# A four-layer convolution and scan kernel: sort comparisons placed by a table, evictions before convolution taps, weight sums in more scan slots, and one activation table for a norm

## The chip, the cores and the metric

The kernel runs on one core of a Trainium2 chip. Its five compute engines appear in the profile as PE (TensorE: matrix products and transposes), DVE (VectorE), ACT (ScalarE), POOL (GpSimd) and SP (SyncE, which here only issues DMAs). The metric is the time of one execution on the device in microseconds. Before the change the median of three executions is 2826.08 us (2825.05 to 2827.95).

## The reference

The input x is one image of 1024 channels and 64 x 64 places, in float32. Four layers follow one another, each added to its input after a group norm over 32 groups:

```python
x = x + L0(gn(x))   # a scan over channels with learned decay
x = x + L1(gn(x))   # 1x1 convolution, 1024 -> 1024, bias
x = x + L2(gn(x))   # gated state-space layer, below
x = x + L3(gn(x))   # 1x1 convolution, 1024 -> 1024, bias
```

Layer 2 is the long one:

```python
xz = silu(in_proj_w @ x + in_proj_b)        # 3072 x 1024 weights
x_ssm, res, gate = split(xz, 3)
xf = silu(conv3(x_ssm))                     # depthwise, 3 taps along the 4096 places
perm = per head, argsort of the score of a Moebius map of the 64 x 64 grid
dt, B, C = split(dbc_w @ xf + dbc_b)        # gathered by perm, as xf is
y = selective_scan(xf[perm], dt, A, B, C)   # two heads, 8 states, 4096 steps
y = y[inverse of perm] * silu(gate) + res
out = silu(out_proj_w @ y + out_proj_b)
```

What is sorted depends on the input `mobius`, so the kernel sorts 4096 keys for each of the two heads on the chip.

## The kernel before, in words

**Products.** A 1024 x 1024 weight matrix times 1024 x 4096 values is worked in four pairs of blocks of 512 columns. Each pair is a 2 x 2 block product in seven products (Strassen's scheme with sums of blocks of the weights and of the values), in two groups of rows, so 14 products a pair. The index `i % 14` in the code is the place of a product in its pair: 0 to 6 for the first group, 7 to 13 for the second. One product is 16 matmuls of 128 x 128 by 128 x 512 (L787) into two PSUM banks of one of two tags, A and B; `put` and `add` carry the banks out (L885 and L889 in the pointwise layer), and a bank can't be written anew before that. The operands of the next pair (b21, b11, b22, then the sums t1 to t4, L745) are made during the last places of a pair, on DVE, and for t2 to t4 on POOL. Sums of weight blocks are made once, on POOL (sum_weights, sum_weights2: L426, L435, L446, L453), stored to DRAM, and loaded again as weights.

**The order of work.** Nearly all stages lie in `tc.manual_schedule` blocks: in these, each engine executes its instructions in the order in which the program issues them. Outside of them the compiler's scheduler chooses. Generators are stepped by hand: after each product, the loop takes one step of whatever runs beside it. So the line at which a step is called sets what stands in front of what on each engine's queue[...].

**The stages**, with their place in the profiled span: layer 0 (0 to 225 us); the pointwise layer 1 (230 to 633, loop at L914); the norm of layer 2 (to 639); the convolution stage, where the first third of the input projection (WX) is followed by the 3-tap convolution, the transposes into token order and the dt/B/C product (639 to 1129, loop at L1108 to L1129, and a tail to 1167); the scan in 74 steps (1180 to 1720, loop L1242 to L1278), with the products of the second third (WR) woven in, 14 a pair again; the gate and output projections (1722 to 2455, two_steps); the norm of layer 3 (to 2474); layer 3 itself (two_steps, to the end).

**The sort** is a bitonic network of 78 comparisons (`compare`, L295 to L319: 11 DVE instructions on tiles of 64 x 128 each), and ten turns of the tile (`turn_over`: two transposes on PE at L329 into a PSUM buffer, and a copy on ACT at L331), after which a permutation goes to DRAM through POOL. It is a generator that yields "compare" or "turn" ahead of each such part; `sort_on` (L373) is called after each product of layer 1 and of the convolution stage, and takes up to n steps. In layer 1 it does so in places 4 to 12, if no sum of weights is under way (`quiet`); in the convolution stage in places 4 to 12, or everywhere from the product 45 on.

**PSUM for transposes.** `ps_tp` (L95) gives out two buffers of one tag, "tp", in turn. The sort's transposes, the norms' small matmuls and the turns of the convolution stage share them: the next user of a buffer waits until the last reader of its former content is done.

**The convolution stage.** After each product, `follow` (L1037) takes two finished blocks of x_ssm through the convolution: `conv` (ACT first tap L973 into a PSUM tile cvp, then two taps on DVE, L976), then silu on ACT (L1047). One call later, `turn` (L986) transposes and multiplies a block by `both` in two halves of two tiles (eight matmuls, L995, into two tp buffers), each half carried out by ACT (l2xt, L997), summed on POOL (L1003) and stored by SP. One of the two blocks turned in a cycle is taken in the middle of the next product (`turn(*due3.pop(0))`), the other in `follow`. ACT also makes the b operands of the next pair (L871), the put and silu of the products' results (L1019, L1028).

**The scan's end.** In each scan step a slot at L1268 lets POOL take one step of the weight sums for WO and W3, except in the places 11 and 12 of a pair of WR; what is left over is done after the last step. Results of WR go through silu and are stored to `res_d` by SP (`activate`, L942 to L948, four at a time). The gate stage begins by reading blocks x_x_b (ACT's queue, L1325), normed into qb (L1332); its first copies out of PSUM are L1497.

**The norm of layer 3** (L1548) has eight aggregations of statistics (L178), two small matmuls (L192, L199), and a logarithm and an exponential for the root (L166, L167).

Of the kernel before, what the change touches and what calls it, by code (L numbers as in the profile page):

```python
# [88 lines left out]
def tile_net(ctx: ExitStack, tc: tile.TileContext, x, par_d, cst_d, w_d, w2_d, dbcw_d, out):  # L89
    nc = tc.nc  # L90
# [29 lines left out]
    def pcol(name, i, rows=P):  # L120
        at = PAR[name].start + i
        return par[:rows, at : at + 1]
# [58 lines left out]
    def group_norm(name):  # L181
        return finish_of(norm_steps(name, *moments(name)))
# [187 lines left out]

    coming = [None]

    def sort_on(quiet, n=2):  # L373

        for _ in range(n):
            was = coming[0]
            if was is None or (was == "compare" and not quiet):
                return
            coming[0] = next(order, None)
            if "turn" in (was, coming[0]):  # L380
                return
# [529 lines left out]
    with tc.manual_schedule(engines={E_.DVE, E_.PE, E_.Pool, E_.Activation}):  # L911
        for i, _ in enumerate(pointwise("l1", W1, "b1", [3, 2] + EARLY, x0_d, x1_d)):
            busy = next(sums, None) if i % 14 < 13 else None
            sort_on(not busy and 3 < i % 14 < 13)  # L914
        for _ in sums:
            pass
    sum_pool.__exit__(None, None, None)
# [32 lines left out]
    with tc.tile_pool(name="l2a", bufs=2) as pa, tc.tile_pool(name="l2a2", bufs=1) as pa2, \  # L950
# [14 lines left out]
        def conv(o, nb):  # L965
            side = nb % 2
            xo = xs[o]
            n = f"{o}_{nb}"
            cv = psa.tile([P, FB], F32, tag="cv", name=f"cvp{n}", bufs=2)
            if side == 1:  # L970
                nc.vector.tensor_copy(carry[:, o, :], xo[:, 2 * FB :])
            at = side * FB
            nc.scalar.activation(cv, xo[:, at : at + FB], AF.Identity, bias=pcol("dwb", o),  # L973
                                 scale=pcol("dww", 3 * o))
            for t in (1, 2):
                nc.vector.scalar_tensor_tensor(cv, xo[:, at + t : at + t + FB], pcol("dww", 3 * o + t), cv,  # L976
                                               ALU.mult, ALU.add)
            if nb == NB - 1:
                e = end[:, o : o + 1]
                nc.vector.tensor_scalar(e, xo[:, 2 * FB : 2 * FB + 1], pcol("dww", 3 * o), pcol("dwb", o),  # L980
                                        ALU.mult, ALU.add)
                nc.vector.scalar_tensor_tensor(e, xo[:, 2 * FB + 1 :], pcol("dww", 3 * o + 1), e,
                                               ALU.mult, ALU.add)
            return o, nb, cv

        def turn(o, nb, cv):  # L986
            pair, side = divmod(nb, 2)
            h, c0 = o // KH, (o % KH) * P
            t0 = nb * FB - 1
            n = f"{o}_{nb}"  # L990
            xt = pa.tile([P, TPB, NV], F32, tag="xt", name=f"l2xt{n}", bufs=3)
            for q0 in (0, 2):
                pt = ps_tp(f"l2pt{n}_{q0}")[:, : 2 * NV]
                for q in range(2):
                    nc.tensor.matmul(pt[:, q * NV : (q + 1) * NV], cv[:, (q0 + q) * P : (q0 + q + 1) * P],  # L995
                                     both[:, o, :], start=True, stop=True)
                nc.scalar.copy(xt[:, q0 : q0 + 2, :].rearrange("p q c -> p (q c)"), pt)  # L997
            if pair not in accs:
                accs[pair] = pa.tile([P, 2 * TPB + 1, HEADS * NF], F32, tag="acc", name=f"acc{pair}", bufs=2)
            acc = accs[pair][:, side * TPB : (side + 1) * TPB, :]  # L1000
            old = acc if nb in done else dbcb.unsqueeze(1).to_broadcast([P, TPB, HEADS * NF])
            done[nb] = True
            nc.gpsimd.tensor_tensor(acc, xt[:, :, P:], old, ALU.add)  # L1003
            xt = xt[:, :, :P]
            if nb == 0:
                nc.sync.dma_start(tok_d[h * N : h * N + P - 1, c0 : c0 + P], xt[1:, 0, :])
                nc.sync.dma_start(tok_rows(t0 + P, TPB - 1, P, c0, h), xt[:, 1:, :])
            else:
                nc.sync.dma_start(tok_rows(t0, TPB, P, c0, h), xt)
# [12 lines left out]
        have, ready, due, due2, due3 = set(), [], [], [], []  # L1022
# [14 lines left out]
        def follow():  # L1037


            made = [conv(*c) for c in due]  # L1040
            for c in due3:
                turn(*c)
            due3[:] = due2
            due2[:] = []
            for o, nb, ps in made:
                cv = pa.tile([P, FB], F32, tag="cv", name=f"cv{o}_{nb}", bufs=4)
                nc.scalar.activation(cv, ps, AF.Silu)  # L1047
                due2.append((o, nb, cv))
            due[:] = ready[:CONVS]
            del ready[:CONVS]  # L1050
# [58 lines left out]
        with tc.manual_schedule(engines={E_.DVE, E_.PE, E_.Pool, E_.Activation}):  # L1109
            nc.sync.dma_start(both[:, :, P:], dbcw_d)  # L1110
            nc.gpsimd.tensor_copy(both[:, :, :P], ident.unsqueeze(1).to_broadcast([P, CT, P]))
            nc.gpsimd.memset(row, 0.0)
            ends, i = iter(()), -1
            for half in run(EARLY + LATE, [WX], normed(norm2), put2a, add2a, before2,
                            last_eng=nc.vector, fine=True, tell=True):
                if half:
                    if due3:
                        turn(*due3.pop(0))
                elif half is False:
                    follow()  # L1120
                if half is not None:
                    continue
                i += 1
                if i > 14 and i % 14 == 4:
                    ends = finish(i // 14 - 1)
                next(ends, None)
                sort_on(3 < i % 14 < 13 or i > 44)
            while coming[0] is not None:
                sort_on(True)  # L1129

            forget(EARLY)
            units = run([3, 2] + EARLY, [WR], normed(norm2), put2b, add2b, before2, fine=True, B=last_B[0])
            total, first, given = NP * 2 * NG * 7, 11, 0

            def next_units(upto):
                nonlocal given
                if given < upto:
                    given += 1
                    next(units, None)

            while ready or due or due2 or due3:
                follow()
                for _ in range(2):
                    next_units(6)
                activate(len(silus))
            for _ in finish(NP - 1):
                pass
# [5 lines left out]
    with tc.tile_pool(name="l2r2", bufs=8) as prg, tc.tile_pool(name="l2g", bufs=5) as pgat, tc.tile_pool(name="l2b", bufs=2) as pb, tc.tile_pool(name="l2h", bufs=1) as ph, \  # L1153
# [88 lines left out]
        with tc.manual_schedule(engines={E_.DVE, E_.PE, E_.Pool, E_.Activation}):  # L1242
            while given < first:
                next_units(total)
            for k in range(4):
                gather(k)
            step_sums(0)
            for k in range(-1, NK + 1):
                upto = first + (k + 2) * (total - first) // (NK + 2)
                turned = turn_rows(k + 1) if k + 1 < NK else None  # L1250
                if k > 0:
                    weigh(k - 1, pgs.pop(k - 1))
                if turned is not None:
                    spread_decay(k + 1, *turned)
                if k + 2 < NK:
                    step_sums(k + 2)
                next_units(upto)
                y = apply(k - 1) if k > 0 else None
                if 0 <= k < NK:
                    pgs[k] = cross(k)  # L1260
                if k + 1 < NK:
                    nc.scalar.activation(decay_[k + 1], decay_[k + 1], AF.Exp)
                if y is not None:
                    scatter(k - 1, y)
                if 3 < k + 4 < NK:
                    gather(k + 4)
                next_units(upto)
                if given // 2 % 14 not in (11, 12):  # L1268
                    next(sums, None)
                if len(silus) > 3:  # L1270
                    activate(4)
            while given < total:
                next_units(total)
            next(units, None)
            while silus:
                activate(4)
            for _ in sums:
                pass  # L1278
# [266 lines left out]

    with tc.manual_schedule(engines={E_.DVE, E_.PE, E_.Pool, E_.Activation}):
        two_steps([job for pair in range(NP) for job in (("gate", WG, pair), ("out", WO, pair))], norm2, x1_d)
    norm3 = group_norm("gn3")  # L1548
    with tc.manual_schedule(engines={E_.DVE, E_.PE, E_.Pool, E_.Activation}):
        two_steps([("last", W3, pair) for pair in range(NP)], norm3, x2_d)  # L1550

# [101 lines left out]
```

## Time and profile before

| | before |
|---|---|
| median of three executions | 2826.08 us |
| profiled execution, its own time | 2827.72 us |
| span of the profile | 2825.9 us |
| PE busy | 2639.0 us (93%) |
| DVE, ACT, POOL busy | 1779.7, 1093.2, 1294.2 us |
| mean granted clock of TensorE | 0.971 |
| PE busy in 230 to 639 (layer 1) | 393.3 of 409 us |
| PE busy in 639 to 1180 (convolution) | 510.3 of 541 us |
| PE busy in 1180 to 1722 (scan) | 526.1 of 542 us |
| PE busy in 1722 to 2455 (gate, out) | 713.8 of 733 us |
| PE busy in 2455 to 2826 (norm, layer 3) | 345.8 of 371 us |

The span runs from the first to the last instruction of one profiled execution. A line of a timeline gives the start, the time, the engine, the line of the program, the operation, what it writes and reads, how many instructions are taken together, and in brackets the time that the engine idled just before and what ended this idling. "issue" means that the engine waited for nothing that the profile shows. A line of the waits gives who waited for whom, the sum in us, the number of times and the longest.

### The profile page before, as it was taken

What the parts mean: (1) busy time and instruction counts of PE and PEld (TensorE: products, weight loads), DVE (VectorE), ACT (ScalarE), POOL (GpSimd) and SP (SyncE); (2) the same over time, 40 slices, a digit from 0 to 9 for tenths busy, and PEclk for the clock granted to TensorE, in tenths of its full rate; (3) what the DMA queues carried; (4) which work ended last, traced back from release to release, by engine and by line L of the source; (5) the groups of instructions that cost most, each with busy time, mean ns of one, the idle gap of its engine ahead of it and who ended that gap; (6) DMA issues with size and microseconds to landing.
All of it is one profiled execution on the core that took longest, in us unless ns stands there. A gap on an engine that the chain in (4) does not pass through costs nothing. (4 is left out here: it accounts for less than half of the span.)

```text
span 2825.9 us, 30977 instructions
## 1 busy us (share of the span) xinstructions
PE 2639.0 (93%) x9586; PEld 1738.7 (62%) x9586; DVE 1779.7 (63%) x3770; ACT 1093.2 (39%) x1839; POOL 1294.2 (46%) x1170
## 2 busy tenths in 40 slices
PE   5778998999999899999999998999999999799999
PEld 4564443444445454444444445888888888688887
DVE  6986775465445454465666664567666675758777
ACT  4773110104546454475656653313232233221220
POOL 4154223421212001168687764556566565455544
PEclk9898999999999999999999998999999999899999
DMA  6335556745433254487778775889899898778896
GB/s 277 134 138 183 190 186 230 225 121 192 153 92 98 89 166 97 139 252 204 212 197 238 243 215 171 227 242 294 230 263 283 240 294 232 234 249 298 302 319 224
DMA packets 423578, 591.47 MB, mean 209 GB/s; under 512 B 149973, under 2 KB 211541, under 8 KB 420342
## 3 DMA queue, kind: packets, MB, share of 16 engines
q1 hardware_dynamic: 297110, 362.09, 41.1%
q10 hardware_dynamic: 93568, 140.52, 14.2%
q0 software_dynamic: 32736, 86.88, 12.0%
q8 instruction: 78, 1.28, 0.2%
q14 instruction: 86, 0.70, 0.1%
HBM read 432.02 MB, written 157.36 MB: 209 GB/s over the span
## 5 line engine op out<-in xcount | busy, mean ns | idle before, releaser
L787 PE MATMUL mm<-t,w 128*128 128x512 f32 x1536 | 687.5, 599 | 0.0
L787 PE MATMUL mm<-b,w 128*128 128x512 f32 x1152 | 524.5, 607 | 14.5 <-issue 9.7
L787 PEld LDWEIGHTS mm<-t,w 128*128 128x128 f32 x1536 | 289.0, 192 | 330.7 <-issue 326.4
L787 PEld LDWEIGHTS mm<-b,w 128*128 128x128 f32 x1152 | 220.2, 195 | 272.0 <-issue 261.6
L1497 ACT COPY qQ<-q_P5P 128x512 f32<-128x512 f32 x48 | 28.1, 586 | 331.1 <-PE q_P5P L1525 248.3
L1003 POOL TENSOR_TENSOR acc<-l2xt,acc 128x136 f32<-128x136 f32 x56 | 27.4, 491 | 277.4 <-ACT l2xt L997 276.5
L976 DVE SCALAR_TENSOR_TENSOR cvp<-xs,par,cvp 128x512 f32<-128x512 f32 x128 | 95.3, 754 | 87.3 <-ACT cvp L973 85.1
L1332 ACT ACTIVATE qb<-x_x_b,gn_bias,gn_r_r 128x512 f32<-128x512 f32 x128 | 96.9, 805 | 92.2 <-DVE qQ L1460 33.7
L426 POOL TENSOR_TENSOR s<-s 128x256 f32<-128x256 f32 (+3 forms) x120 | 128.8, 1080 | 7.9
L1225 ACT COPY g<-py 8x512 f32<-8x512 f32 x146 | 83.9, 575 | 119.2 <-PE py L1222 117.7
L1231 POOL DMA_INDIRECT y_d<-y,dst x74 | 75.6, 1021 | 115.3 <-ACT y L1227 47.9
L1027 DVE TENSOR_TENSOR xs<-mm,xs 128x512 f32<-128x512 f32 x64 | 41.6, 684 | 135.9 <-PE mm L787 135.9
L1213 DVE TENSOR_TENSOR E<-E,pg 128x512 f32<-128x512 f32 x74 | 50.8, 687 | 109.1 <-PE pg L1205 107.3
L745 POOL TENSOR_TENSOR t<-b,t 128x512 f32<-128x512 f32 x72 | 94.3, 1336 | 50.2 <-DVE t L745 50.1
L885 DVE SCALAR_TENSOR_TENSOR image<-mm,par,image 128x512 f32<-128x512 f32 x64 | 47.1, 745 | 104.9 <-PE mm L787 104.9
L995 PEld LDWEIGHTS l2pt<-both,cv 128*128 128x128 f32 x512 | 77.9, 192 | 53.8 <-issue 27.3
L1328 POOL TENSOR_TENSOR t_t<-qt 128x512 f32<-128x512 f32 x24 | 30.4, 1268 | 162.9 <-DVE qt L1328 94.9
L1525 PE MATMUL q_P1P<-t_b,wq_P1P 128*128 128x256 f32 x384 | 94.5, 392 | 11.0 <-ACT qZ L1497 8.2
L995 PE MATMUL l2pt<-both,cv 128*128 128x162 f32 x512 | 85.0, 307 | 20.3 <-ACT l2xt L997 18.2
L1328 POOL TENSOR_TENSOR t_t<-qt,t_t 128x512 f32<-128x512 f32 x48 | 73.0, 1522 | 53.9 <-DVE qt L1328 53.6
L1525 PE MATMUL q_P4P<-t_t,wq_P4P 128*128 128x256 f32 x384 | 92.3, 384 | 2.2 <-POOL qD L1412 2.2
L1412 DVE TENSOR_TENSOR qQ<-qQ,qV 128x512 f32<-128x512 f32 x48 | 70.9, 1477 | 33.9 <-POOL qZ L1412 33.5
(372 smaller groups left out, 5972.5 us busy)
## 6 DMA issues: line engine op xcount, KB each, us to landing
w<-s_d SPq DMA_DIRECT2D x96, 512.0 KB, 3.7
w<-in_w_dram SPq DMA_DIRECT2D x72, 512.0 KB, 3.5
x_x_b<-x_d ACTq DMA_DIRECT2D x32, 1024.0 KB, 6.9
image<-x_d SPq DMA_DIRECT2D x12, 2048.0 KB, 12.0
wq_P6P<-s_d SPq DMA_DIRECT2D x84, 256.0 KB, 4.2
wq_P7P<-s_d SPq DMA_DIRECT2D x84, 256.0 KB, 7.8
wq_P5P<-s_d SPq DMA_DIRECT2D x84, 256.0 KB, 4.6
wq_P3P<-s_d SPq DMA_DIRECT2D x84, 256.0 KB, 3.3
```

Source lines behind the costliest of these rows:

```text
L426: eng.tensor_tensor(out, a, b, ALU.subtract)
L745: eng.tensor_tensor(B[name][k], B[one][k], B[two][k], ALU.subtract)
L787: nc.tensor.matmul(to[o], w[:, k, o * P : (o + 1) * P], B[name][k], start=(fresh and k == 0), stop=(k == KH - 1), skip_group_check=True)
L976: nc.vector.scalar_tensor_tensor(cv, xo[:, at + t : at + t + FB], pcol("dww", 3 * o + t), cv, ALU.mult, ALU.add)
L995: nc.tensor.matmul(pt[:, q * NV : (q + 1) * NV], cv[:, (q0 + q) * P : (q0 + q + 1) * P], both[:, o, :], start=True, stop=True)
L1213: nc.vector.tensor_tensor(Ef, Ef, pg, ALU.mult)
L1225: nc.scalar.copy(rows[k + 1][h * LC : h * LC + S, :DH], py[h * LC : h * LC + S])
L1231: nc.gpsimd.indirect_dma_start(out=y_d[:, :], out_offset=bass.IndirectOffsetOnAxis(ap=dst_[:, k : k + 1], axis=0), in_=y[:, :], in_offset= ...
L1328: eng.tensor_tensor(to, a, b, ALU.subtract)
L1332: nc.scalar.activation(tile_of(j, name)[:, k], held[j, "x", name][:, k], AF.Identity, bias=norm[1][:, ct : ct + 1], scale=norm[0][:, ct : ...
L1412: eng.tensor_tensor(x, x, y, ALU.add)
L1525: nc.tensor.matmul(ps[:, o, :], w[:, k, o * P : (o + 1) * P], rhs[:, k, :], start=(new and o == 0 and k == 0), stop=(k == 1), skip_group_c ...
```

## The change

It has four parts.

1. `sort_on(quiet, n)` no longer counts steps but comparisons: it goes on until n comparisons are made, and then stops in front of the next one. A turn is let through whatever n is (before, only in the places named above), and still ends the call. The number n comes from a table by the product's place in its pair: in layer 1 (0, 0, 0, 0, 3, 2, 1, 2, 1, 3, 3, 3, 0, 0), if no sum is under way; in the convolution stage (0, 0, 0, 1, 3, 1, 0, 2, 0, 2, 3, 3, 0, 0), in all pairs. Before it was two in each of places 4 to 12. The sum over a pair is 18 in layer 1, as before, and 15 in the convolution stage, in place of 18.
2. In `follow`, the turns come ahead of the convolutions, so on ACT the evictions L997 stand in front of the first tap L973.
3. The slot for weight sums in the scan is open in place 11 too, so the last chunk of the sums lies within the scan, ahead of the last stores of res_d.
4. At the norm of layer 3, one table set that holds both functions is loaded explicitly, and the norm is moved into the block with the order of the program, so its eight aggregations follow the last statistics in one row.

The number of matmuls, of comparisons and of DMAs stays; ACT has one table load fewer. On PE the only difference in order is that five of the sort's transposes stand one product earlier.

```diff
--- before.py
+++ after.py
@@ -370,12 +370,15 @@
 
     coming = [None]
 
-    def sort_on(quiet, n=2):
-
-        for _ in range(n):
+    def sort_on(quiet, n):
+
+
+        while coming[0] is not None:
             was = coming[0]
-            if was is None or (was == "compare" and not quiet):
-                return
+            if was == "compare":
+                if n == 0 or not quiet:
+                    return
+                n -= 1
             coming[0] = next(order, None)
             if "turn" in (was, coming[0]):
                 return
@@ -911,7 +914,7 @@
     with tc.manual_schedule(engines={E_.DVE, E_.PE, E_.Pool, E_.Activation}):
         for i, _ in enumerate(pointwise("l1", W1, "b1", [3, 2] + EARLY, x0_d, x1_d)):
             busy = next(sums, None) if i % 14 < 13 else None
-            sort_on(not busy and 3 < i % 14 < 13)
+            sort_on(not busy, (0, 0, 0, 0, 3, 2, 1, 2, 1, 3, 3, 3, 0, 0)[i % 14])
         for _ in sums:
             pass
     sum_pool.__exit__(None, None, None)
@@ -1037,9 +1040,9 @@
         def follow():
 
 
-            made = [conv(*c) for c in due]
             for c in due3:
                 turn(*c)
+            made = [conv(*c) for c in due]
             due3[:] = due2
             due2[:] = []
             for o, nb, ps in made:
@@ -1124,9 +1127,9 @@
                 if i > 14 and i % 14 == 4:
                     ends = finish(i // 14 - 1)
                 next(ends, None)
-                sort_on(3 < i % 14 < 13 or i > 44)
+                sort_on(True, (0, 0, 0, 1, 3, 1, 0, 2, 0, 2, 3, 3, 0, 0)[i % 14])
             while coming[0] is not None:
-                sort_on(True)
+                sort_on(True, 1)
 
             forget(EARLY)
             units = run([3, 2] + EARLY, [WR], normed(norm2), put2b, add2b, before2, fine=True, B=last_B[0])
@@ -1265,7 +1268,7 @@
                 if 3 < k + 4 < NK:
                     gather(k + 4)
                 next_units(upto)
-                if given // 2 % 14 not in (11, 12):
+                if given // 2 % 14 != 12:
                     next(sums, None)
                 if len(silus) > 3:
                     activate(4)
@@ -1545,7 +1548,8 @@
 
     with tc.manual_schedule(engines={E_.DVE, E_.PE, E_.Pool, E_.Activation}):
         two_steps([job for pair in range(NP) for job in (("gate", WG, pair), ("out", WO, pair))], norm2, x1_d)
-    norm3 = group_norm("gn3")
+        nc.scalar.preload_act_table_set("natural_log_exp_and_others")
+        norm3 = group_norm("gn3")
     with tc.manual_schedule(engines={E_.DVE, E_.PE, E_.Pool, E_.Activation}):
         two_steps([("last", W3, pair) for pair in range(NP)], norm3, x2_d)
 
```

## The prediction

> **What bounds the kernel.** I read the page, then PE's waits, then the timeline around each long wait.
>
> ```profile
> span 2825.9 us, 30977 instructions
> PE 2639.0 (93%) x9586; PEld 1738.7 (62%) x9586; DVE 1779.7 (63%) x3770; ACT 1093.2 (39%) x1839; POOL 1294.2 (46%) x1170
> ```
> PE sets the end; the change removes no matmul, so it can only move some of PE's 187 us of idle time. Who ends it:
>
> ```profile
> PE gn_pg L192 <- DVE gn_mv L178: 26.6, 4, 11.6
> PE l2pt L995 <- ACT l2xt L997: 18.2, 10, 5.5
> PE mm L787 <- issue: 9.7, 1, 9.7
> PE sort L329 <- ACT l2xt L997: 9.6, 3, 3.7
> PE q_P1P L1525 <- ACT qZ L1497: 8.2, 1, 8.2
> PE l2pt L995 <- ACT lines L331: 1.4, 1, 1.4
> ```
> (us in all, times, longest.) The "issue" wait is one event. PE's, DVE's and POOL's timelines there:
>
> ```profile
> 442.60 5.93 PE L787 MATMUL mm<-b,w 128*128 128x512 f32 x7 [9.74 <-issue]
> ```
> ```profile
> 427.78 2.50 DVE L310 TENSOR_TENSOR swap<-lines 64x64 f32<-64x64 f32 x2
> 430.21 1.30 DVE L311 TENSOR_TENSOR swap<-lines 64x64 f32<-64x64 f32 x1
> 440.38 0.21 DVE L311 TENSOR_TENSOR swap<-lines 64x64 f32<-64x64 f32 x1
> 441.82 0.68 DVE L889 TENSOR_TENSOR image<-mm,image 128x512 f32<-128x512 f32 x1
> ```
> ```profile
> 435.05 4.92 POOL L745 TENSOR_TENSOR t<-b,t 128x512 f32<-128x512 f32 x4
> ```
> Two compares stand between the combinations L745 and the adds L889 that free a PSUM bank. While POOL works (424.06 to 440), a compare's instruction takes 1.30 us instead of 0.21: the two last 14.04 us instead of 3.5, and PE waits 9.74 for the bank.
>
> The convolution stage, second pair of column blocks, on PE:
>
> ```profile
> 830.54 1.37 PE L995 MATMUL l2pt<-both,cv 128*128 128x162 f32 x8 [1.96 <-ACT l2xt L997]
> 835.63 0.47 PE L329 MATMUL sort<-cst,lines 64*128 64x64 f32 x2 [3.73 <-ACT l2xt L997]
> 836.03 5.92 PE L787 MATMUL mm<-b,w 128*128 128x512 f32 x8
> 843.72 3.60 PE L787 MATMUL mm<-b,w 128*128 128x512 f32 x8
> 849.74 0.82 PE L995 MATMUL l2pt<-both,cv 128*128 128x162 f32 x4 [1.87 <-ACT l2xt L997]
> ```
> PE waits for the evictions L997 that free the "tp" buffers, and afterwards runs slow: eight products in 5.92 us, then in 3.60. Every wait of about 2 us or more costs some 2 us again.
>
> End of the scan, on SP, ACT and PE:
>
> ```profile
> 1723.33 6.74 SPq L453 DMA_DIRECT2D s_d<-s  x4
> 1730.16 3.33 SPq L947 DMA_DIRECT2D res_d<-rg  x2
> ```
> ```profile
> 1736.28 0.81 ACT L1332 ACTIVATE qb<-x_x_b,gn_bias,gn_r_r 128x512 f32<-128x512 f32 x1 [9.51 <-DMA res_d<-rg]
> ```
> ```profile
> 1739.83 5.42 PE L1525 MATMUL q_P1P<-t_b,wq_P1P 128*128 128x256 f32 x12 [8.17 <-ACT qZ L1497]
> ```
> The last weight sum's four stores occupy SP's queue for 6.74 us ahead of the last two stores of res_d, for which the gate stage waits. At the third norm, ACT loads two tables:
>
> ```profile
> 2467.59 1.28 ACT L166 ACT_TABLE_LOAD   x1 [2.50 <-DVE gn_mv L178]
> 2470.78 1.28 ACT L167 ACT_TABLE_LOAD   x1
> ```
>
> **What the Trainium skill says.** "TensorE: Matmul & The Clock Gate" (What's actually happening): an idle window of about 3.4 us sets the array to half clock. The trace agrees in kind (5.92 against 3.60), though waits of 1.9 us already do it. "GPSIMD Engine Reference" (1. Specifications): GpSimd shares its SBUF interface with VectorE, with contention when a VectorE instruction has two SBUF inputs; the compares do, and the trace shows 1.30 against 0.21. "ScalarE: Activation LUTs" (What ACT_TABLE_LOAD costs): about 1283 ns plus a drain of 1380; the trace shows 1.28 for the load and, from it to the next activation's start, nothing more.
>
> **The change, part by part.** Sums are made against the profiled execution (2827.72 us, span 2825.9) and carried to the median 2826.08, 0.06% lower, as differences.
>
> *Compares by place, pointwise stage.* The 78 compares stay (11 VectorE instructions, 1.75 us each undisturbed). Place 12 of a cycle loses its two, so after L745 (ends 427.86) the adds L889 start at about 427.9 instead of 441.82 and end (four adds with their statistics) before PE's next bank is needed at 432.86: −9.74, and the slow clock behind it (32 matmuls in 16.66 us, 13.73 elsewhere) −2.93. Places 9 to 11 get a third compare. Ahead of this stall the compares at 406.10 took 10.55 under POOL's sum (405.59 to 414.14); a third ends at 418.4 instead of 416.65. PE's next group starts near 419.0, so it costs 0 to 0.3. Transposes move one product earlier, 0.3 us of PE each, nothing lost. Bounds: −12.7 to −4 (the third compare itself slowed under a sum, up to 8.5 us of POOL work). I take −12.5.
>
> *Convolution stage: compares by place and evictions first.* In follow(), the L997 evictions come ahead of cvp L973 and its taps. I replayed it by hand with the trace's durations (L973 1.47 a pair, L997 0.74 a pair, taps L976 1.54 a pair, L1047 0.60, L331 0.35). The 1.96 goes, the 3.73 becomes about 3.2, the 1.87 about 0.7, and PE reaches the next turn some 3.3 us earlier. There it meets something new: the sort's transposed block holds one of the two tp buffers until ACT's copy L331, queued behind xs, evictions, cvp, cv and four b fills L871 (2.92). That chain is about 10.0 us instead of 8.1, so the turn in the middle of place 10 waits about 4 us, plus 2 of clock. So pairs two and three come to about 0 each (−2 to +2), pair one, which had less to gain, to +2. The waits at 1011 and 1024 (0.50, 1.41) go, pair four gains 0.8 of its 1.43, the tail 1.4 of its 5.52: 2 − 1.9 − 0.8 − 1.4 ≈ −2; I take −1.5. Bounds: +8 if the new wait comes everywhere and nothing goes; −38 if all waits but the tail's go (23.3) with the nine slow windows at 1.7.
>
> *One chunk more inside the scan.* Steps in which POOL does a combination and a large sum (9.2 us) right behind a 7.5 us step make PE wait for cd. Before: steps 19 and 61 (1.99, 3.18), and 34 and 38 (0.29, 1.86). With the sums shifted, by counting, steps 40 and 58, perhaps 18. −1.8 (−5 to +3).
>
> *End of the scan.* The sum of chunk 7 (stores L453, 6.74 us of SP) is issued before the last res_d stores, which then go at about 1718.7 to 1722.0 and land near 1726 instead of 1735.8. Then the fetch of x_x_b bounds: issued at about 1722.7, 6.9 us to land, and two steps. The same boundary after the third norm shows a wait of 2.79 where this one has 8.17. The three waits here (2.24, 2.03, 8.17) fall from 12.44 to about 5: −7.4, and one slow window (1.7): −9 (−12 to −5). All other stores and loads keep their order on SP; P1P's loads are far ahead.
>
> *One table for the norm.* L167's load leaves the chain: −1.28. But in one block, the eight aggregations L178 (0.37 us, 0.29 apart) all follow the last statistics instead of between them; the last ends at 2469.45 instead of 2468.40: +1.05. The load at 2467.59 was hidden behind VectorE; the one that stays is too. −0.25 (−1.5 to +1).
>
> Sum: −12.5 − 1.5 − 1.8 − 9 − 0.3 = −25.1, so 2801.0.
>
> **Rivals.** (1) *The convolution's waits go as well.* For it: evictions come first on ACT and L331's chain may be shorter than I replayed. Against: the second tp buffer. Half of the 38: 2826.1 − 23.6 − 20 ≈ 2782. (2) *Half of the gains move elsewhere*: the third compare is slowed under a sum (−7.5 in place of −12.5), the fetch of x_x_b eats half of the scan's end (−5), the convolution loses 2: −12, 2814. For it: margins near nothing at 418.4 against 419.0. (3) *Slower: the tp buffer.* If the wait for L331 in place 10 of the first three pairs is a whole product (9.1 us) with 1.7 of clock, that is +32 against −23.6: 2835. It decides from 8 us a pair on; my replay has 6 with other waits gone, and before, the largest wait for L331 was 1.4. (4) *Not as it says*: compares are also held up elsewhere, and the end-of-scan wait is for another transfer: 2822 to 2828.
>
> **How the numbers follow.** Forecast 0.50 (2790 to 2812 its own range), rival one 0.20, two 0.21, three 0.05, four 0.04. A range of 2782 to 2818 leaves out half of one's lower part, three and four. Faster by over 0.2% (5.7 us; about what a measurement can tell here) is forecast, one and two: 0.91; within it 0.04; slower 0.05.
>
> **What would show it.** Right: no wait "mm <- issue" of 9.7, adds L889 directly behind L745; res_d's last stores ahead of L453's; the 8.17 for qZ down to about 3; one table load at gn3 and a first wait there near 12.6; in the convolution, new waits "l2pt <- ACT lines/turned L331" of about 4 in places 10. Wrong: no such wait (then rival one), a wait for mm near 425 or in another cycle, an unchanged wait for qZ.

## The result, and the profile after

The changed kernel takes 2806.0 us (median of four runs, 2804.22 to 2809.79) against 2825.57 for the kernel before beside it: a ratio of 0.9926, 95% interval 0.9911 to 0.994, or 17 to 25 us less. The forecast was 2801.0 us, 25.1 less than before, with a range of 2782 to 2818. The direction and the range held; the gain was a fifth smaller.

The page of the changed kernel, its head:

```profile
span 2802.9 us, 30986 instructions
PE 2631.1 (94%) x9586; PEld 1733.6 (62%) x9586; DVE 1777.2 (63%) x3770; ACT 1091.3 (39%) x1838; POOL 1290.3 (46%) x1170
```

Every busy time is nearly what it was; PE works 2631 of 2803 us instead of 2639 of 2826. Of the 23 us by which the span is shorter, 15 were idle time of PE. The other 8 are busy time, and as the matmuls are as many as before (9586), they are matmuls that ran faster. PE's waits of the changed kernel (us in all, times, longest; its line numbers are 3 higher than before's behind the sort):

```profile
PE l2pt L998 <- ACT turned L331: 11.5, 3, 3.8
PE pg L1208 <- POOL cd L1194: 9.1, 5, 2.7
PE sort L329 <- ACT l2xt L1000: 8.6, 3, 3.4
PE l2pt L998 <- ACT l2xt L1000: 8.5, 9, 4.1
PE q_P1P L1528 <- issue: 6.3, 2, 3.6
PE sort L329 <- DVE turned L319: 2.0, 1, 2.0
```

The 9.7 us for a PSUM bank ("mm <- issue") and the 8.2 for qZ are gone. In their place PE waits three times 3.8 us for the sort's copy L331; before, it waited for this copy twice, 1.4 and 0.8 us.

To see where the time went, I take the start of the same PE instruction in both traces at the border of each stage:

| stage, up to | before, us | after, us | difference | forecast |
|---|---|---|---|---|
| layer 0 (unchanged), first product of layer 1 | 230.62 | 228.51 | −2.1 | 0 |
| layer 1, first product of WX | 408.57 | 399.13 | −9.4 | −12.5 |
| convolution stage, last l2pt | 524.16 | 522.47 | −1.7 | −1.5 |
| scan, first P1P of the gate | 559.34 | 560.28 | +0.9 | −1.8 |
| end of the scan, second half of that P1P | 17.14 | 9.30 | −7.8 | −9 |
| gate and output (unchanged), last wait for POOL | 711.66 | 709.03 | −2.6 | 0 |
| norm of layer 3, its first P1P | 22.49 | 21.82 | −0.7 | −0.25 |
| layer 3, to the end of PE's last matmul | 345.56 | 345.43 | −0.1 | 0 |

The differences sum to −23.6. Behind PE's last matmul the span goes on for 6.96 us instead of 6.39, which gives the 23.0 of the span. This tail is 6.39 or 6.40 us in all eight kernels of this study without the new slot for sums and 6.94 to 6.96 in the six with it, so the slot costs 0.6 us there; the cause stays open. The rows for unchanged stages show what one profile can't tell. In the fourteen kernels of this study the gate and output stage, the same in all of them, takes from 706.7 to 715.5 us. In one comparison the reason can be seen: a wait of PE at 2297.45 was 2.48 us before and the fourteen matmuls behind it took 4.8 us; after the change it is 1.63 and they take 3.1. So −2.1 and −2.6 are not put down to the change; its own stages sum to −18.7, within the interval of the timed runs.

### The profile page after: what moved, and what is told of

It is laid out like the page before. It is cut to its first block, busy times and chain, and to the rows that moved or that the text cites. A ratio compares the mean times of both kernels' runs of the same rounds, so it can differ in the third digit from the quotient of the medians.

```text
span 2802.9 us, 30986 instructions
## 1 busy us (share of the span) xinstructions
PE 2631.1 (94%) x9586; PEld 1733.6 (62%) x9586; DVE 1777.2 (63%) x3770; ACT 1091.3 (39%) x1838; POOL 1290.3 (46%) x1170
## 3 DMA queue, kind: packets, MB, share of 16 engines
q8 instruction: 78, 1.28, 0.2%
## 4 chain that ended last, share of the span: by engine, by line
PE 50%; DMA 3%; DVE 2%; POOL 2%; issue 1%; ACT 1%; DVEq 0%; POOLq 0%; ACTq 0%
PE mm L790 10%; PE q_P7P L1528 5%; PE q_P5P L1528 5%; PE q_P3P L1528 5%; PE q_P6P L1528 5%; PE q_P4P L1528 5%; PE q_P1P L1528 5%; PE q_P2P L1528 4%; PE pg L1208 2%; PE py L1225 2%; DMA qD<-x_d 1%; POOL s L429 1%; PE pr L1184 1%; DMA y_d<-y,dst 0%; POOL t L748 0%
```

## The experiments

Each kernel below is the kernel before (or the changed one) with the edit shown. For all of them I took the same borders, from the profiled run; totals are medians and ratios to before's runs on the same chip.

| kernel | layer 1 | convolution | scan | its end | norm | total, ratio (interval) |
|---|---|---|---|---|---|---|
| before | 408.6 | 524.2 | 559.3 | 17.1 | 22.5 | |
| whole change | 399.1 | 522.5 | 560.3 | 9.3 | 21.8 | 2806.0, 0.9926 (0.9911 to 0.994) |
| table of layer 1 alone | 397.5 | 524.6 | 559.3 | 17.2 | 22.5 | 2814.5, 0.9939 (0.9915 to 0.9963) |
| no compares in place 12 | 395.6 | 523.7 | 561.9 | 17.3 | 22.5 | 2815.7, 0.9958 (0.9943 to 0.9972) |
| evictions first alone | 408.5 | 528.0 | 562.7 | 17.3 | 22.5 | 2833.1, 1.0020 (1.0012 to 1.0029) |
| convolution's table alone | 408.8 | 524.1 | 560.2 | 17.2 | 22.5 | 2828.1, 1.0002 (0.9991 to 1.0014) |
| slot for sums alone | 408.7 | 524.3 | 566.6 | 9.3 | 22.5 | 2819.4, 0.9968 (0.9948 to 0.9987) |
| one table, norm in block, alone | 408.3 | 523.5 | 562.7 | 17.2 | 21.8 | 2827.7, 0.9997 (0.9988 to 1.0006) |
| whole, norm out of the block | 397.5 | 521.8 | 559.8 | 9.3 | 21.2 | 2802.7, 0.9918 (0.9901 to 0.9935) |
| whole, early copy | 396.5 | 501.9 | 563.5 | 9.4 | 21.8 | 2787.3, 0.9859 (0.9842 to 0.9875) |
| the same, one compare moved | 397.4 | 494.4 | 559.5 | 9.5 | 21.8 | 2778.1, 0.9826 (0.9797 to 0.9855) |
| before, early copy | 408.6 | 516.4 | 559.0 | 17.3 | 22.5 | 2816.7, 0.9966 (0.9957 to 0.9976) |
| before, early copy, evictions first | 408.6 | 513.1 | 559.8 | 17.4 | 22.5 | 2816.2, 0.9959 (0.9948 to 0.9970) |
| all together | 395.2 | 493.0 | 564.5 | 9.3 | 21.2 | 2779.1, 0.9829 (0.9813 to 0.9845) |

Where an edit doesn't touch them, layer 1 repeats within 0.5 us, the convolution stage within 1.1, the scan's end within 0.3 and the norm within 0.1. The scan doesn't: 559.0 to 562.7 without the new slot, 559.5 to 566.6 with it. Two profiled runs were the slowest of their kernels (evictions first alone, slot for sums alone). Where the length of a stage leaves doubt, I therefore also give PE's idle time in it, that is its length less PE's busy time; what is left is matmuls that ran slower or faster.

### Layer 1: the compares of place 12

The table of layer 1 alone, with the new `sort_on` in this layer:

```diff
-            sort_on(not busy and 3 < i % 14 < 13)
+            sort_on(not busy, (0, 0, 0, 0, 3, 2, 1, 2, 1, 3, 3, 3, 0, 0)[i % 14])
```

> Only the table of the pointwise layer; the convolution stage keeps two steps in places 4 to 12. Theory (the compares of place 12, slowed by POOL, hold the bank): the 9.7 us wait for a bank near 442 is gone, the first matmul behind the second norm comes 9 to 12 us earlier than in before, and the total falls by 9 to 12 us. Rival (the stall only moves into places 9 to 11): the total falls by less than 5 us and PE shows another wait for a bank. What is seen as a wait for the sort's transposes in the layer (2.0 us after the whole change, 0.4 before) depends, by the theory, on when a sum's chunk on POOL meets the compare ahead of it, so it may be anything between 0.4 and 2.

Only place 12 emptied, its two compares moved to places 4 and 9, with the old `sort_on`:

```diff
-            sort_on(not busy and 3 < i % 14 < 13)
+            sort_on(not busy and 3 < i % 14 < 12, 3 if i % 14 in (4, 9) else 2)
```

> Before, with one edit: the pointwise layer makes no compares in place 12; one more each in places 4 and 9. Theory (the compares of place 12 alone make the 9.7 us wait): as much as the whole table of this layer gives, -9 to -13 us, with the wait for the bank gone. Rival (the other places of the table matter as well): at most half of it.

The layer became 11.1 us shorter with the table and 13.0 us with place 12 alone; the wait for the bank is gone in both, and in all five kernels with the table the layer is 396.5 to 399.1 us. So the compares of place 12 made the stall, the rest of the table with its new rule for turns adds nothing, and it loses 1 to 3.5 us. Where it loses them is seen on PE of the changed kernel, first the old place of the stall, then a later pair:

```profile
423.90 20.76 PE L790 MATMUL mm<-b,w 128*128 128x512 f32 x48
...
488.63 0.30 PE L329 MATMUL sort<-cst,turned 128*64 128x128 f32 x1 [2.01 <-DVE turned L319]
488.76 8.73 PE L790 MATMUL mm<-b,w 128*128 128x512 f32 x16
```

At 423.90 the three products run through where 9.74 us were idle. But at 488.63 the sort's transposes wait for a compare, and the product behind them takes 8.73 us. In the other four kernels with the table this product takes 7.03, so the 1.7 us of slow clock belong to this run and not to the table. VectorE and POOL at that place:

```profile
480.17 1.65 DVE L310 TENSOR_TENSOR swap<-turned 128x32 f32<-128x32 f32 x2
488.39 0.18 DVE L319 TENSOR_TENSOR turned<-turned,swap 128x32 f32<-128x32 f32 x1
```
```profile
481.74 6.45 POOL L429 TENSOR_TENSOR s<-s 128x896 f32<-128x896 f32 x3
```

One compare lasts 8.4 us because a sum's chunk (POOL, 479.58 to 488.19) runs through it. The transposes' place was the same before, where the like compare took 6.9 us and PE waited 0.4. In the five kernels with the table PE waited 1.4 to 2.0 us there, with place 12 alone 0.29 (0.14 and 0.15, the second shown):

```profile
487.49 0.30 PE L329 MATMUL sort<-cst,turned 128*64 128x128 f32 x1 [0.15 <-DVE turned L319]
```

In that kernel POOL began its chunk 2.58 us ahead of the compare, before 2.38 us, and 0.59 to 1.36 us in the five with the table. In the last kernel below, again with place 12 alone emptied, it was 3.30 us, and PE did not wait. The smaller this lead, the more of the chunk is still to run when the compare starts. Why the lead is smaller with the table is left open.

### The convolution stage: two rules that hurt alone

Evictions first, without the table:

```diff
         def follow():
-            made = [conv(*c) for c in due]
             for c in due3:
                 turn(*c)
+            made = [conv(*c) for c in due]
```

> Only the order in follow: evictions ahead of convolution taps, with the old places of the compares. Theory (evictions on ACT end PE's waits): the waits of 1.96 and 1.87 in pairs two and three shrink below 0.8, the 3.7 of the sort's transposes becomes 3.2 to 3.4, no new wait for the sort's copy as long as the turn takes place in the old product; in all -4 to -10 us in the convolution stage. Rival (the order alone is neutral because the taps come later and the copy with them): within 2 us of before.

The table, without evictions first:

```diff
-                sort_on(3 < i % 14 < 13 or i > 44)
+                sort_on(True, (0, 0, 0, 1, 3, 1, 0, 2, 0, 2, 3, 3, 0, 0)[i % 14])
```

> Only the table of the convolution stage, with the old order in follow and the old rule in the pointwise layer. Theory (the table moves the turns one product earlier, and the copy then stands behind the next pair's b fills): the waits of 3.7 for the sort's transposes stay, the 1.96 stays, and new waits for the sort's copy of about 2 us and more come in the first three pairs; the stage is 0 to 12 us longer than in before. Rival (the table relieves VectorE and so PE): the stage becomes shorter by 3 us or more.

Both expectations were wrong. Evictions first alone made the stage 3.8 us longer (1.2 of it idle time of PE, from 30.5 to 31.7) and the kernel slower by 0.2%; expected were 4 to 10 us less, or by the rival no change. PE of that kernel, second pair:

```profile
834.32 0.47 PE L329 MATMUL sort<-cst,lines 64*128 64x64 f32 x2 [2.30 <-ACT l2xt L997]
856.39 0.82 PE L995 MATMUL l2pt<-both,cv 128*128 128x162 f32 x4 [3.84 <-ACT turned L331]
```

The transposes' wait falls from 3.73 to 2.30, further than expected; the 1.96 ahead of it, which was to shrink below 0.8, stays. And the wait for the sort's copy comes here too, with the turns of the sort in their old product. So it is the order in follow that makes it, not the table. The table alone was expected to bring this wait and a stage up to 12 us longer. It has no such wait; its transposes wait longer:

```profile
834.90 0.47 PE L329 MATMUL sort<-cst,lines 64*128 64x64 f32 x2 [4.80 <-ACT l2xt L1010]
```

and the 1.96 ahead of them is gone. PE idles 2.7 us less, its matmuls take 2.7 us more, and the stage is unchanged (524.1). Together, in the changed kernel:

```profile
823.95 0.47 PE L329 MATMUL sort<-cst,lines 64*128 64x64 f32 x2 [3.39 <-ACT l2xt L1000]
835.96 0.82 PE L998 MATMUL l2pt<-both,cv 128*128 128x162 f32 x4 [0.56 <-ACT l2xt L1000]
844.59 1.45 PE L998 MATMUL l2pt<-both,cv 128*128 128x162 f32 x4 [3.84 <-ACT turned L331]
```

These are the waits that the prediction replayed (3.2, 0.7, 4). On ACT, ahead of the last:

```profile
841.48 2.91 ACT L874 ACTIVATE b<-image,gn_bias,gn_r_r 128x512 f32<-128x512 f32 x4
844.30 0.24 ACT L331 COPY turned<-sort 128x128 f32<-128x128 f32 x1
```

The copy needs 0.24 us. It reads transposes that PE made at 823.95, and starts 20 us later, behind four fills for the next pair. Until then one of two tp buffers is taken, and each turn has only the other: its second half waits for the eviction of its first (0.56), and the last for the copy.

### The tp buffer held by the sort

If that is the cause, the copy has to be issued sooner; nothing else needs to change. In the middle of a product, where the loop already calls turn, I let the sort take its copy if its transposes are out:

```diff
+            tile_out[0] = True       # in turn_over, behind the transposes
             yield "turn"
             nc.scalar.copy(new.rearrange("p c w -> p (c w)"), pt[:w, : 2 * rows])
+            tile_out[0] = False
...
                 if half:
+                    if tile_out[0]:
+                        sort_on(True, 0)
                     if due3:
                         turn(*due3.pop(0))
```

> The whole change, and in the convolution stage the copy of the sort's turned tile is issued on ACT in the middle of the product behind the transposes, ahead of the next pair's b fills, and no longer after it. Theory (the second tp buffer is held by the sort's transposes until this copy): the three new waits of 3.84 for it vanish with about 1.7 us of slow clock each; the convolution stage is 10 to 17 us shorter than after the whole change, and the total 2789 to 2797. Rival (the wait is for the evictions that stand ahead in ACT's queue, and not for the place of the copy): less than 4 us.

The convolution stage fell by 20.6 us against the changed kernel, more than expected, and the kernel to 2787.3. On ACT and PE of this kernel:

```profile
820.84 0.26 ACT L334 COPY turned<-sort 128x128 f32<-128x128 f32 x1
```
```profile
816.25 0.47 PE L331 MATMUL sort<-cst,lines 64*128 64x64 f32 x2 [3.37 <-ACT l2xt L1004]
```

The copy comes 4.6 us behind its transposes. In pairs two and three the wait of 3.37 is the only one left: with the 3.84 both waits of 0.56 went too. Three pairs by 4.96 are 14.9 us, less 0.38 that stays in pair one; the other 6.1 of the 20.6 are matmuls that ran slowly before. My expectation had counted the 3.84 alone.

The same edit on the kernel before (there as `sort_on(True, 1)`, one step of the old kind), and with evictions first on top:

> Before, with one edit: in the convolution stage the copy of the sort's turned tile is issued in the middle of the product behind the transposes. Theory (the tp buffer held by the sort made the 0.56, 1.87, 0.77 and 1.41 of before): these vanish, the 1.96 and 3.7 stay; with slow clock the stage is 10 to 18 us shorter than in before. Rival (those waits are the order of evictions and taps on ACT, as the change's second part would have it): less than 5 us.

> The same one edit, and evictions ahead of taps in follow, with the old places of the compares. Theory (evictions first lost 4 us in the stage because the copy came later; with the copy early nothing of that is left): 1 to 6 us shorter in the stage than with the early copy alone, from the 3.7 of the transposes falling to 2.3. Rival (evictions first costs by itself, since the taps and so the next turn come later): longer than with the early copy alone.

Before's waits of 0.56, 1.87, 0.77 and 1.41 all vanish. Pair one shows this with the transposes in their old place: they stand behind the same product and wait 2.17 us as before, and the 0.56, 1.87 and 0.77 behind them are gone. The stage is 7.8 us shorter, less than expected, because new waits come in the later pairs. One sort step more is taken early in each turn, so with the old rule the compares and transposes fall into other products, and the 1.96 and 3.7, which were to stay, give way to others; the largest new wait is

```profile
827.91 0.31 PE L331 MATMUL sort<-cst,lines 64*128 64x64 f32 x2 [4.62 <-DVE xs L1022]
```

With evictions first on top of it the stage is 3.3 us shorter again (513.1), 2.2 of it idle time of PE. The size is as expected, the place is not: the transposes of pair one wait 0.75 us instead of 2.17, and a turn in the tail 4.11 instead of 5.52. The totals of these two do not tell them apart (0.9966 and 0.9959). So what evictions first is worth depends on what stands beside it. In idle time of PE it loses 1.2 us alone and 0.8 behind the table (27.8 to 28.6), and gains 2.2 behind the early copy. The 1.6 us by which the stage is shorter behind the table (524.1 to 522.5) are matmuls that ran faster in that run.

### The wait that remained

The 3.37 is for evictions (L1004) that stand on ACT behind a silu, which waits for an add on VectorE, which stands behind two compares of place 7:

```profile
814.55 1.33 ACT L1035 ACTIVATE xs<-xs,par 128x512 f32<-128x512 f32 x2 [3.40 <-DVE xs L1034]
```

One of the two compares moved to place 6:

```diff
-                sort_on(True, (0, 0, 0, 1, 3, 1, 0, 2, 0, 2, 3, 3, 0, 0)[i % 14])
+                sort_on(True, (0, 0, 0, 1, 3, 1, 1, 1, 0, 2, 3, 3, 0, 0)[i % 14])
```

> As the version with the early copy of the turned tile, with one of the two compares of place 7 in the convolution stage moved to place 6, where VectorE idles 2.1 us. Theory (the adds that ACT's queue waits for, ahead of the evictions, stand behind two compares): the wait of 3.37 for the sort's transposes in pairs two and three falls to about 1.5, each with up to 2.5 us of slow clock; the convolution stage is 3 to 9 us shorter than with the early copy alone, the total 2779 to 2785. Rival (the wait is set by the evictions' own chain): within 2 us of it.

```profile
812.14 0.33 PE L331 MATMUL sort<-cst,lines 64*128 64x64 f32 x2 [1.66 <-ACT l2xt L1004]
```

The wait halves (pair one's goes from 1.78 to 0.75), and the stage gains 7.5 us: the waits for the transposes fall by 4.5 and two in pair four (1.0) go; a new wait of 0.39 comes, and matmuls that ran faster give the other 2.4. The total of 2778.1 lies just below the 2779 to 2785 expected.

### The end of the scan

```diff
-                if given // 2 % 14 not in (11, 12):
+                if given // 2 % 14 != 12:
```

> Only the slot for sums in place 11 of the scan. Theory (the last chunk's stores held up the last stores of res_d): the three waits at the scan's end fall from 12.4 to about 6 us, the second half of P1P comes 7.5 to 9.5 us earlier, and the total falls by 7 to 10 us; the scan itself stays within 2 us. Rival (the gain is that of other slots in the scan): the scan's end shows less than half of this.

The end of the scan takes 9.3 to 9.5 us in all six kernels with this edit, and 17.1 to 17.4 in all without: −7.8, the most even gain of the study. The kernel gains 0.3%. The scan itself was expected to stay within 2 us; the profiled run, the slowest of its six (2828.21), shows 7.2 us more there. In the changed kernel, on SP and PE:

```profile
1703.43 6.55 SPq L950 DMA_DIRECT2D res_d<-rg  x6
```
```profile
1710.39 5.68 PE L1528 MATMUL q_P1P<-qb,wq_P1P 128*128 128x256 f32 x16 [2.24 <-ACT qb L1335]
1719.69 6.30 PE L1528 MATMUL q_P1P<-t_b,wq_P1P 128*128 128x256 f32 x16 [3.61 <-issue]
```

The six res_d stores go without a sum's store between them; the stores of the last sum went at 1671.09, 32 us earlier. The three waits of 12.44 us are now two of 5.85. The 9.3 holds a wait of 3.61 at the spot where the norm of layer 3 has one of 2.8 before and 2.7 after.

### The norm of layer 3

```diff
+        nc.scalar.preload_act_table_set("natural_log_exp_and_others")
-    norm3 = group_norm("gn3")
+        norm3 = group_norm("gn3")
```

> Only the table and the norm within the program's order. Theory: 1.28 us of table load go, 1.05 us of aggregations at the end come; from the last matmul of the output stage's wait for POOL to the second half of P1P -0.9 to +0.5 us, the total within 1 us of before. Rival (the load was all that mattered): -1.3 us there.

And the whole change with the norm outside of the block again, so that the scheduler places the aggregations:

> The whole change, with the norm of layer 3 out of the block again (the one table set stays), so that the aggregations stand between the statistics. Theory: the last aggregation ends about 1 us earlier and the norm's matmul with it; -0.8 to -1.3 us at this norm against the whole change, below what the totals can tell. Rival: the scheduler's aggregations delay VectorE's sums, and nothing is gained.

From PE's last wait for POOL to the norm's first matmul it is 16.97 us before, 17.59 and 17.60 with the norm in the block, 16.98 with it outside; from that matmul to the first product 5.52 before and 4.23 to 4.25 with one table, in or out. So one table is worth 1.29 us, and the block costs 0.62, less than the 0.8 to 1.3 expected. The last aggregations of the two, on VectorE, of the changed kernel and of the one with the norm outside:

```profile
2444.29 1.97 DVE L178 BATCH_NORM_AGGREGATE gn_mv<-stats 128x2 f32<-128x48 f32 x8
```
```profile
2440.97 0.37 DVE L178 BATCH_NORM_AGGREGATE gn_mv<-stats 128x2 f32<-128x48 f32 x1
```

The totals don't tell one table alone from before (0.9997), nor the two places of the norm in the whole change from each other (0.9926 and 0.9918).

### All together

The version with the early copy and the moved compare, with place 12 alone emptied in layer 1 and the norm out of the block:

> The best of the parts together: as the version with the early copy and one compare moved, and with two edits more: the pointwise layer keeps two steps in places 4 to 11 with one more in 4 and 9 and none in 12, and the norm of layer 3 stands outside of the block. Theory: the pointwise layer is 1 to 2.5 us shorter (13.0 against 9.4 to 12.1 us saved in it), the last aggregation is 0.6 us earlier; in all -1 to -3 us against the version with one compare moved, 2775 to 2777, which the totals hardly tell. Rival (the pointwise layer's gain depends only on when a sum's chunk meets a compare): no gain there, 2777 to 2779.

2779.1 us (2770.61 to 2780.03), 0.9829 with 0.9813 to 0.9845: 1.7% less than before and 1% less than the changed kernel, and not to be told from the version ahead of it (0.9826). Expected were 2775 to 2777, so the total does not show the gain of the two edits. By the borders layer 1 gained 2.2 us and the norm 0.6, as the theory had it, and the scan took about 5 us more, where such a difference decides nothing; the profiled run (span 2768.8) was the fastest of its five.

## Why the prediction was right, point by point

The changed stages sum to −18.7 us against −25.1. Layer 1, the scan and the scan's end fell short by 7.0 us together, and no term went far the other way; the range was wide enough for that.

**Layer 1, −12.5 forecast, −9.4 measured** (−9.4 to −12.1 over five kernels). The mechanism held: place 12 alone gives 13.0. What failed is that everything else in the layer was put at next to nothing. The step "Transposes move one product earlier, 0.3 us of PE each, nothing lost" is true of those that moved: by the traces these are four of the ten turns, not five, two of them in this layer, and they wait for nothing. The loss is at transposes whose place stayed. The compare ahead of them now meets more of a chunk on POOL, and PE waits 2.01 us instead of 0.44; in this run 1.7 of slow clock came on top. I had priced slowed compares for the third compare ahead of the stall (there it cost nothing, as forecast) and not for the compares ahead of transposes.

**Convolution stage, −1.5 forecast, −1.7 measured.** The net is right and so are its terms: 3.39 against 3.2, 0.56 against 0.7, 3.84 against 4. By pairs it is +2.4, −0.7, +0.6 and −1.8, and −2.2 in the tail, against +2, 0, 0, −2.7 and −1.4. What the prediction did not see is that the waits of 0.56 and 1.87 of before had the same cause as the new one. It named the held tp buffer for the new wait only, and gave the old ones to the order on ACT. The early copy removed them in both kernels. The order has a part in the 1.87 alone, which evictions first without the early copy brings to 0.56.

**Scan, −1.8 forecast, +0.9 measured.** The length can't decide this: the stage repeats no better than 559.0 to 562.7 without the edit. The six kernels with it average 562.4, the eight without 560.6; a gain of 1.8 is not seen. But the waits for cd, on which the term rests, say that the counting of steps failed. Of the kernel before, to be set against the 9.1 us of the changed kernel:

```profile
PE pg L1205 <- POOL cd L1191: 7.3, 4, 3.2
```

The forecast had these waits in steps 40 and 58 and perhaps 18. In the changed kernel they are in steps 13 and 14 (2.68, 2.28), 40 (1.85), 61 and 62 (1.70, 0.58): step 40 came, 58 did not, 61 only shrank, and 13 and 14 were not foreseen. PE's idle time in the scan averages 18.6 us over the six kernels with the slot and 16.9 over the eight without.

**End of the scan, −9 forecast, −7.8 measured.** The mechanism held: the first qb that waits for a late block of x_x_b starts 5.80 us behind the first P1P instead of 13.59 (1716.19 in the changed kernel, 1736.28 before), and that is the 7.8. Forecast were 7.4 from the waits, and 1.7 from one slow window less. PE's three waits fell by 6.6 only, and the sixteen matmuls ahead of the last one by 1.3, but this split says little: in the eight kernels without the slot the sixteen take 5.5 to 7.0 us and the last wait 9.8 to 8.2, and the end takes 17.1 to 17.4 all the same. The wait takes up what the matmuls leave. What failed is the slow window as a sure gain. The sixteen matmuls behind the last wait take 6.30 us after and 6.28 before; in three of the six kernels with the slot they take 3.69, in none of the eight without. (The sign that the prediction names, res_d's last stores ahead of the sum's, contradicts its working: the sum's stores went first.)

**Norm, −0.25 forecast, −0.7 measured.** The table was right to the hundredth (1.29 against 1.28). The aggregations cost 0.62 and not 1.05; that between the statistics they had taken VectorE's time as well, so that moving them gave part of it back, fits but was not tested. The first wait, forecast near 12.6, is 13.90, because the eight matmuls ahead of it took 1.97 us in this run and 3.62 before; from border to border the block shows as 0.62.

**The slow clock.** The prediction lets every wait of about 2 us or more cost some 2 us again. That is not so every time: behind the same wait of 2.17 us the same eight matmuls took 3.62 us in one run and 1.97 in another (last section), and the product behind layer 1's wait of 2.01 took 8.73 in one and 7.03 in another. It is a cost that may come, and no fixed term of a sum.

**Rivals.** The first (the convolution's waits go as well, 2782) did not come by this change; what the prediction set against it, the second tp buffer, is what held it back, since the early copy on top of the change brought 2787. The second (2814; its terms give 2813) was partly true in layer 1, but not by the third compare. The third (slower by the tp buffer) is what evictions first does by itself: 1.0020. In the whole change the table removes before's 1.96, 0.50 and 1.41 and so pays for it. The 23.3 us of waits in the lower bound for the convolution stage leave out three of 0.56.

## What to carry to other kernels

When a wait names an eviction, ask who else holds buffers of that tag. Here a copy of 0.24 us, issued late on ACT, cost the changed kernel 20 us in the convolution stage; in the kernel before, 7.3 of the 9.5 us of waits that vanished with the early copy had been put down to the evictions. Before reordering a queue, write down for each shared buffer at which instruction it comes free; an edit that is harmful alone can turn into a gain once the held buffer is released, though here that gain is seen in PE's idle time (2.2 us) and not in the totals. And take the term of a step from a stage border in several kernels that don't touch it: here one profile tells about 1 us in the stages with even borders, and nothing below 4 to 9 us in the scan and in the gate stage. There the list of waits, or the idle time, tells more than the length.

## What the runs showed of the hardware that was not expected

A compare's instruction (64 partitions, two inputs in SBUF) that falls into a POOL instruction lasts until that one ends: 1.29 us beside L745's (1.23 us each), 2.09 beside L426's (2.13 each), 0.21 alone. In the trace of before, of the compare at 406.10, four slowed instructions end within 0.3 us of the end of a POOL instruction (those of its group of three taken as evenly long). Not all are held: L313 of that compare starts at 411.99, within 0.1 us of the start of a POOL instruction, and takes 0.21. An add of VectorE with one input from PSUM was not held: 0.68 us at 427.27 in the changed kernel, with POOL at work from 423.55 to 439.5.

PE's slow clock follows waits of 2 us in some executions and not in others. The wait for POOL at the end of the output stage is 2.17 to 2.18 us in the traces of before, of the changed kernel and of the one with the norm outside. The eight matmuls behind it take 3.62, 1.97 and 3.22 us, at a granted clock of 0.58, 1.00 and 0.59 over that stretch. PE was busy without a gap for 9 us ahead of the first and 12 us ahead of the last. The untouched gate and output stage differs by 8.8 us over fourteen profiles, about as much as one of the parts of this change is worth; that such chance windows make up all of it is my reading, and was looked at in two of the profiles only.
